# One square root a turn in the last stage of a convolution and attention kernel

## The chip, the core and the metric

The kernel runs on one core of a Trainium2 chip. A core has a matrix engine (PE, with weight loads shown apart as PEld), a vector engine (DVE), an activation engine (ACT), a general engine (POOL), a queue engine (SP) and 16 DMA engines. Each engine runs its own list of instructions in order, and waits on semaphores that the others raise. The metric is the device time of one execution in microseconds (us).

## What is computed

The input has 4 images of 64 channels and 256 x 256 pixels. Two layers follow each other. Only the end of the second one matters here: linear attention along the columns, then a small network at each pixel.

```
def _ln(x, g, b):
    m = x.mean(-1, keepdims=True)
    v = jnp.mean((x - m) ** 2, -1, keepdims=True)
    return (x - m) / jnp.sqrt(v + EPS_LN) * g + b
...
hc = _ln(h.swapaxes(1, 2), cn_g, cn_b)
h = h + _lin_attn(hc, col_wq, ..., col_bo).swapaxes(1, 2)
f = _ln(h, fn_g, fn_b)
f = gelu(f @ w1.T + b1) @ w2.T + b2
return moveaxis(h + f, -1, 1)
```

So `h` is normalized twice over its 64 channels: once before the attention, and once, after the attention has been added, before the network. Each normalization needs one square root and one reciprocal per pixel. In the attention, queries and keys have one channel for each of 4 heads; `elu(.) + 1` is applied to both, and elu needs an exponential.

## The kernel before, in words

The program is one function with several stages. Everything here happens in the last, `stage_d`. It works on 32 groups (4 images x 8). A group is a tile `h` of 128 partitions x 32 columns x 2 row halves x 64 channels, which `load` fetches with 4 DMAs of 512 KB on SP's queue (L1172); four such tiles exist at a time.

Four pieces of work run side by side, each for another group. In turn `n`:

- `scores(n+1)` transposes `h` in 8 pieces (`up`, L1210, copied by ACT at L1212), multiplies by the weights of queries and keys (L1219), and brings the products back with two transposes on DVE (L1224). The mean is inside the weights, so only the root is still to be applied: L1249. Then L1250 adds the bias, `feature` takes the smaller of the value and zero (L695) and its exponential (L696), L1258 makes `f`, and L1260 makes `kz`, the keys times the root.
- `result(n)` starts with the product of `kz` and `h` (L1271), goes through a chain of small steps (L1283 to L1299), and adds the attention to `h`: PE at L1305 and L1308, DVE at L1311. Then it normalizes the new `h` into four tiles `xf`.
- `turn` and `first`, for the group before, transpose a piece of `xf` (L1330, copied by ACT at L1332), multiply by the first weights (L1341) and apply the Gelu (L1343, four per piece).
- `second` transposes the piece of `h`, adds the second product (L1355 and L1358), and DVE evicts the sum to `st` (L1359). After 8 pieces four DMAs on POOL's queue write `st` out (L1365).

A turn has 8 steps, `r` = 0 to 7. In each step PE is given `turn(i+2)`, `first(i+1)`, a part of `scores`, a part of `result`, `second(i)`, and a part of `scores` and of `result` again, where `i = 8(n-1) + r`. `scores` and `result` are generators, and each `yield` ends a part. The first piece of `xf` of group `n` is transposed in step 6 of turn `n`; its second tile is needed from step 0 of the next turn.

PE's order is this order, written out by hand (`manual_schedule`). The orders of DVE and ACT are made by a planner that takes ready instructions by priority with its own estimate of the times. PSUM has 6 buffers called `mm` for nearly all products, and 2 called `sm`. A product that takes an `mm` buffer waits until the engine that reads the buffer's last content is done. So PE can be held by an eviction that has nothing to do with its own work.

The sum of a normalization is made by `spread`: for each of 2 tiles of 16 pixels x 64 channels the row sum (L1181, DVE), the centred values (L1183, DVE), their squares (L1185, ACT) and the sum of squares (L1189, DVE). `rstd` takes the root (L1194, ACT) and the reciprocal (L1196, DVE). ACT holds one table of functions at a time: going from Gelu to the root, to the exponential, or back shows in the trace as its own instruction, ACT_TABLE_LOAD.

In a turn before the change there are three calls of `rstd`: one of 64 values a partition for the scores, at the end of `scores`, and one of 32 for each half of the result.

Of the kernel before, what the change touches and what calls it, by code (L numbers as in the profile page):

```python
# [18 lines left out]
LN_S = 1.0 / C  # L19
# [230 lines left out]
def kernel(ctx: ExitStack, tc: tile.TileContext, x, packs, fd, out, off):  # L250
    nc = tc.nc
    B = x.shape[0]
    V, S, T, G, SY = nc.vector, nc.scalar, nc.tensor, nc.gpsimd, nc.sync
# [24 lines left out]
    eps_t = const.tile([128, 1], F32, name="eps_t")  # L278
# [18 lines left out]
    def bc(ap, n):  # L297

        return ap.unsqueeze(2).to_broadcast([ap.shape[0], ap.shape[1], n])
# [27 lines left out]
    p = sp1.enter_context(tc.tile_pool(name="pst", bufs=2))  # L327
    p1 = sp1.enter_context(tc.tile_pool(name="pst1", bufs=1))
# [110 lines left out]
    rss, l4s = {}, {}  # L439
# [699 lines left out]
    def stage_d():  # L1139
        with ExitStack() as cs:  # L1140
            p = cs.enter_context(tc.tile_pool(name="pd", bufs=2))
            p1 = cs.enter_context(tc.tile_pool(name="pd1", bufs=1))
# [25 lines left out]
            def load(b, g):  # L1168
                h = p.tile([128, 32, 2, C], F32, name="h", bufs=4)
                for rh in (0, 1):  # L1170
                    for j in (0, 1):
                        SY.dma_start(h[:, 16 * j:16 * j + 16, rh, :], hd[b, rh * 128:(rh + 1) * 128, :, 2 * g + j, :])  # L1172
                return h

            def spread(h, ks, v):

                xcs, sqs = [], []
                for k in ks:
                    src = h[:, 8 * k:8 * k + 8].rearrange("p c a e -> p (c a) e")
                    s1 = p.tile([128, 16], F32, tag="ln_s", name="ln_s")  # L1180
                    V.tensor_reduce(s1, src, AX.X, ALU.add)  # L1181
                    xc = p.tile([128, 16, C], F32, tag="xc", name="xc")
                    V.scalar_tensor_tensor(xc, bc(s1, C), -LN_S, src, ALU.mult, ALU.add)  # L1183
                    sq = p.tile([128, 16, C], F32, tag="ln_sq", name="ln_sq")
                    S.activation(sq, xc, AF.Square)  # L1185
                    xcs.append(xc)
                    sqs.append(sq)
                for i, k in enumerate(ks):
                    V.tensor_reduce(v[:, 16 * i:16 * i + 16], sqs[i], AX.X, ALU.add)  # L1189
                return xcs  # L1190

            def rstd(v, n):
                s3 = p.tile([128, n], F32, tag="ln_d", name="ln_d")
                S.activation(s3, v, AF.Sqrt, bias=eps_t, scale=LN_S)  # L1194
                s4 = p.tile([128, n], F32, tag="ln_r", name="ln_r")
                V.reciprocal(s4, s3)  # L1196
                return s4

# [3 lines left out]
            def scores(n):  # L1202
                h = hs[n]
                qp = p1.tile([128, 32, 32], F32, name="qp")
                v1 = p1.tile([128, 64], F32, name="v1")
# [24 lines left out]
                for r in range(8):  # L1230
                    if r == 0:
                        spread(h, (0, 1), v1[:, 0:32])
                    if r == 4:
                        back(0, qk)
                        qk = sm()
                    score(r, xT, qk)
                    if r < 7:
                        xT = up(r + 1)
                    if r == 3:
                        spread(h, (2, 3), v1[:, 32:64])  # L1240
                    yield
                    if r == 1:
                        yield
                        yield

                back(1, qk)
                rs = rstd(v1, 64)
                u = qp[:, :, 0:16].rearrange("p c (r k) -> p c r k", r=2)
                V.tensor_tensor(u, u, bc4(rs, 2, 8), ALU.mult)  # L1249
                V.tensor_tensor(u, u, cbq.unsqueeze(1).unsqueeze(1).to_broadcast([128, 32, 2, 8]), ALU.add)  # L1250
                e = feature(p1, u, [128, 32, 2, 8])
                yield
                f = p1.tile([128, 2, 2, 32, 4], F32, name="f")
# [6 lines left out]
                V.tensor_tensor(kz.rearrange("p r (c h) -> p r c h", h=4), f[:, :, 1], rs.rearrange("p (c r) -> p r c", r=2).unsqueeze(3).to_broadcast([128, 2, 32, 4]), ALU.mult)  # L1260
                fks[n] = f, kz

            def result(n):
                h = hs[n]
# [36 lines left out]
                for rh in (0, 1):  # L1301
                    ts = [mm() for g in range(4)]
                    for g in range(4):
                        r = slice(g * 32, g * 32 + 32)
                        T.matmul(ts[g], one[g * 32:g * 32 + 1, :], K("colbo8")[g * 32:g * 32 + 1, :], start=True, stop=False)  # L1305
                    for g in range(4):
                        r = slice(g * 32, g * 32 + 32)
# [3 lines left out]
                        V.tensor_tensor(hh, ts[g].rearrange("p (c e) -> p c e", c=8), hh, ALU.add)  # L1311
                    yield
                for hf in (0, 1):
                    v2 = p.tile([128, 32], F32, name="v2")
                    xcs = spread(h, (2 * hf, 2 * hf + 1), v2)
                    yield
                    rs = rstd(v2, 32)
                    for k in (0, 1):
                        xf = p.tile([128, 8, 2, C], F32, name="xf", bufs=6)
                        V.tensor_tensor(xf.rearrange("p c a e -> p (c a) e"), xcs[k], bc(rs[:, k * 16:k * 16 + 16], C), ALU.mult)  # L1320
                        xfs[n, 2 * hf + k] = xf
                    yield

            def turn(i):

# [9 lines left out]
            def first(i):  # L1335
                xT = xTs.pop(i)
                hgs[i] = []
                for k in (0, 1):
                    for rh in (0, 1):
                        t = mm()  # L1340
                        T.matmul(t, w1[rh * 64:(rh + 1) * 64, k * 128:(k + 1) * 128], xT[rh * 64:(rh + 1) * 64], start=True, stop=True)  # L1341
                        g = p.tile([128, 512], F32, tag=f"hg{rh}{k}", name=f"hg{rh}{k}")
                        S.activation(g, t, AF.Gelu, bias=b1[:, k:k + 1])  # L1343
                        hgs[i].append(g)
# [22 lines left out]

            seq = [(b, g) for b in range(B) for g in range(8)]
            N = len(seq)
            hs, fks, xfs, xTs, hgs, sts = {}, {}, {}, {}, {}, {}  # L1370
            hs[0] = load(*seq[0])
            with tc.manual_schedule(engines={mybir.EngineType.PE}):
                for n in range(-1, N + 1):
                    if 0 <= n + 2 < N:
                        hs[n + 2] = load(*seq[n + 2])
                    gs = scores(n + 1) if n + 1 < N else iter(())
                    gr = result(n) if 0 <= n < N else iter(())
                    for r in range(8):
                        i = 8 * (n - 1) + r
                        if 0 <= i + 2 < 8 * N:  # L1380
                            turn(i + 2)
                        if 0 <= i + 1 < 8 * N:
                            first(i + 1)
                        next(gs, 0)
                        next(gr, 0)
                        if 0 <= i < 8 * N:
                            second(i)
                        next(gs, 0)
                        next(gr, 0)
                    _steps(gs, gr)  # L1390

    stage_d()


# [18 lines left out]
```

## Time and profile before

| what | value |
|---|---|
| time, median of 3 runs | 8800.12 us (8797.13 to 8805.94) |
| the profiled execution's own time | 8803.6 us, span 8801.8 us |
| its granted PE clock, mean | 0.969 of full speed |
| PE busy | 8178.1 us (93%) |
| DVE busy | 5927.4 us (67%) |
| ACT busy | 4601.7 us (52%) |
| last stage | from about 6690 us to the end |
| 30 turns in it, 6824.20 to 8728.50 us | 1904.3 us, 63.48 us each |

How to read it: a busy PE is not a PE at its peak, since a matmul that waits inside the pipeline counts as busy. Shares of the whole span mix stages with different limits; what matters here is one turn of the last stage. Times in the trace are counted from the start of the span. Releasers ("<-DVE kz L1260") say which instruction ended a wait. The granted clock is 1.00 at full speed and 0.50 at half.

### The profile page before, as it was taken

To read this page: it belongs to the slowest core of one execution; us is meant where nothing else is said; L and a number is where in the kernel's file an instruction comes from. 1 tells how busy PE (TensorE), PEld (TensorE's weight loads), DVE (VectorE), ACT (ScalarE), POOL (GpSimd) and SP (SyncE) were. 2 spreads that over 40 slices of the span, in tenths; PEclk is the share of its full clock that TensorE was granted. 3 is DMA by queue.
4 is the path that set the end of the run, shared out by engine and by line. 5 is a ranking of instruction groups with operands and counts; after the bars stand their busy time and mean duration, and the time that the engine had idled before them with its cause. 6 is when DMAs were issued, how large, how long until landed. Compare 5 with 4: busy or idle time off the path is not lost. (4 is left out here: it accounts for less than half of the span.)

```text
span 8801.8 us, 143151 instructions
## 1 busy us (share of the span) xinstructions
PE 8178.1 (93%) x57518; PEld 4216.6 (48%) x57518; DVE 5927.4 (67%) x8506; ACT 4601.7 (52%) x7779; POOL 1205.2 (14%) x1828
## 2 busy tenths in 40 slices
PE   8999999699999998999999999999997999999998
PEld 6777777344444443333333344444443444444443
DVE  7766666377777774222222288888886888888886
ACT  4455455455555553222222266666663777777776
POOL 1111111212222221000000011111110010101011
PEclk9999999699999999999999999999997999999999
DMA  7777777799999998888888755555552232323232
GB/s 161 161 188 187 182 182 180 193 347 388 396 391 388 386 387 320 298 296 298 296 297 298 273 184 172 173 168 167 169 158 63 59 77 58 77 58 77 58 77 39
DMA packets 1258502, 1832.48 MB, mean 208 GB/s; under 512 B 335600, under 2 KB 1040112, under 8 KB 1196656
## 3 DMA queue, kind: packets, MB, share of 16 engines
q1 hardware_dynamic: 1053296, 1034.63, 39.0%
q0 software_dynamic: 204544, 788.69, 28.0%
q8 instruction: 456, 7.47, 0.3%
q14 instruction: 206, 1.69, 0.1%
HBM read 967.65 MB, written 788.53 MB: 200 GB/s over the span
## 5 line engine op out<-in xcount | busy, mean ns | idle before, releaser
L915 DVE TENSOR_TENSOR y<-ge,mm 128x512 f32<-128x512 f32 (+1 forms) x640 | 406.3, 635 | 1212.8 <-ACT ge L914 1212.8
L882 PE MATMUL mm<-t,w 128*128 128x512 f32 (+1 forms) x2560 | 1094.1, 566 | 18.8 <-DMA t<-td 18.8
L914 ACT ACTIVATE ge<-mm 128x512 f32<-128x512 f32 (+1 forms) x640 | 354.9, 555 | 1253.5 <-PE mm L889 1253.5
L775 PE MATMUL mm<-gp,wc 128*64 128x510 f32 (+1 forms) x3072 | 702.7, 596 | 90.8 <-DVE xm L785 51.4
L620 PEld LDWEIGHTS mm<-wqk,gp 128*128 128x128 f32 x6144 | 728.7, 197 | 99.2 <-issue 61.5
L882 PEld LDWEIGHTS mm<-t,w 128*128 128x128 f32 x2560 | 455.4, 190 | 647.5 <-issue 437.0
L620 PE MATMUL mm<-wqk,gp 128*128 128x128 f32 x6144 | 762.3, 282 | 1.1 <-POOL gp L589 0.9
L1341 PE MATMUL mm<-xfT,w 64*128 64x512 f32 x2048 | 620.9, 642 | 51.1 <-ACT hg L1343 26.8
L1343 ACT ACTIVATE hg<-mm,b 128x512 f32<-128x512 f32 x1024 | 634.1, 688 | 53.2 <-PE mm L1341 51.5
L830 ACT COPY tb<-mm 128x512 f32<-128x512 f32 x512 | 300.7, 588 | 632.4 <-PE mm L824 632.1
L889 PE MATMUL mm<-t,w 64*64 64x504 f32 (+1 forms) x5120 | 575.6, 555 | 0.0
L824 PE MATMUL mm<-xl,pack_c 64*128 64x512 f32 x2048 | 513.5, 601 | 8.1 <-ACT xl L812 4.7
L1358 PE MATMUL mm<-hg,pack_d 128*64 128x512 f32 x2048 | 505.8, 615 | 0.0
L775 PEld LDWEIGHTS mm<-gp,wc 128*64 128x64 f32 x3072 | 277.8, 137 | 470.5 <-issue 333.3
L316 ACT ACTIVATE ln_sq<-xn 128x1024 f32<-128x1024 f32 x256 | 274.3, 1072 | 365.4 <-DVE xn L314 365.3
L1365 POOL DMA_DIRECT2D out_dram<-st x128 | 209.1, 1638 | 1756.3 <-DVE fe L695 1543.6
L318 DVE TENSOR_REDUCE ln_v<-ln_sq 128x16 f32<-128x1024 f32 x256 | 312.0, 1219 | 186.0 <-ACT ln_sq L316 186.0
L970 PE MATMUL mm<-ya,pack_e 128*64 128x512 f32 x1024 | 381.2, 616 | 11.2 <-DMA ya<-yd 11.2
L828 DVE COPY tb<-mm 128x512 f32<-128x512 f32 x512 | 345.0, 685 | 24.0 <-PE mm L824 18.5
L1359 DVE TENSOR_SCALAR st<-mm,pack_d 128x512 f32<-128x512 f32 x256 | 281.1, 1098 | 117.9 <-PE mm L1358 117.6
L1341 PEld LDWEIGHTS mm<-xfT,w 64*128 64x128 f32 x2048 | 225.1, 192 | 276.1 <-issue 125.7
L1185 ACT ACTIVATE ln_sq<-xc 128x1024 f32<-128x1024 f32 x256 | 273.0, 1067 | 132.1 <-DVE xc L1183 132.1
(458 smaller groups left out, 15283.8 us busy)
## 6 DMA issues: line engine op xcount, KB each, us to landing
t<-td SPq DMA_DIRECT2D x256, 1152.0 KB, 9.9
td<-tb POOLq DMA_DIRECT2D x144, 1024.0 KB, 15.6
td<-tb POOLq DMA_DIRECT2D x288, 512.0 KB, 13.9
yd<-y POOLq DMA_DIRECT2D x128, 1152.0 KB, 10.1
ya<-yd SPq DMA_DIRECT2D x192, 512.0 KB, 5.7
xs<-in_x_dram SPq DMA_DIRECT2D x128, 512.0 KB, 6.8
projd<-pj POOLq DMA_DIRECT2D x256, 256.0 KB, 6.0
gp<-projd SPq DMA_DIRECT2D x128, 512.0 KB, 9.5
```

Of the source, the lines that this page charges most:

```text
L620: T.matmul(qp[:, k * 128:(k + 1) * 128], gp[:, 2 * i + k // 2, at + dx:at + dx + 128], wqk[:, dx, :], start=(dx == 0), stop=(dx == 2))
L775: T.matmul(tv[i * 64:(i + 1) * 64, :, o], wc[2 * pr + i][:, dx, :], gps[i][:, 2 * r:2 * r + 2, i_], start=(dx == 1), stop=False, skip_grou ...
L824: T.matmul(t, inT[q, hf * 128:(hf + 1) * 128], xls[b // 2, s][q, :, 2 * y:2 * y + 2].rearrange("p f y t -> p f (y t)"), start=True, stop=True)
L828: V.tensor_copy(o, i_)
L882: T.matmul(t[:, :n], w[:, 0:128], x_[:, c, :], start=True, stop=False, skip_group_check=True)
L889: T.matmul(t[po:po + 64, :n].rearrange("p (n c) -> p n c", c=64)[:, :, o], w[q:q + 64, 128:192], x_[q:q + 64, c, i_], start=False, stop=Tr ...
L914: S.activation(ge[:, :n], ts[0][k][:, :n], AF.Gelu)
L915: V.tensor_tensor(y[:, c, :].rearrange("p n c -> p (n c)"), ge[:, :n], ts[1][k][:, :n], ALU.mult)
L970: T.matmul(t[b * 64:(b + 1) * 64, :], owT, ya[:, :, 2 * r:2 * r + 2, b * 64:(b + 1) * 64].rearrange("p f y t -> p y f t"), start=True, sto ...
L1341: T.matmul(t, w1[rh * 64:(rh + 1) * 64, k * 128:(k + 1) * 128], xT[rh * 64:(rh + 1) * 64], start=True, stop=True)
L1343: S.activation(g, t, AF.Gelu, bias=b1[:, k:k + 1])
L1358: T.matmul(y[rh * 64:(rh + 1) * 64, :], w2[:, k, :], hg[k * 2 + rh], start=False, stop=(k == 1), skip_group_check=True)
```

## The change

`scores` and `result` no longer take roots. A tile `v1` of 128 values a partition holds the sums of squares of a turn: 64 for the scores of group `n+1`, and 64 for the result of group `n`. `root(n, ...)`, called in step 5 of turn `n` before that step's parts of `scores` and `result`, takes one root and one reciprocal of all 128 values.

The sums for the scores of group `n+2` are made in steps 6 and 7 of turn `n`, after everything else of these steps, so that they are complete one turn ahead; those of group 0 come before the loop. The sums for the result stay in steps 3 and 4, and the centred values are written straight into `xf`. All four `xf` tiles are multiplied by the root in place, in step 5, after `root`. There `result` has two empty parts before. No DMA is added or removed, and PE has the same products in the same order.

```
-            def spread(h, ks, v):
-
-                xcs, sqs = [], []
-                for k in ks:
+            def spread(h, ks, v, xcs=None):
+
+                sqs = []
+                for i, k in enumerate(ks):
...
-                    xc = p.tile([128, 16, C], F32, tag="xc", name="xc")
+                    xc = xcs[i].rearrange("p c a e -> p (c a) e") if xcs else p.tile([128, 16, C], F32, tag="xc", name="xc")
...
-            def rstd(v, n):
-                s3 = p.tile([128, n], F32, tag="ln_d", name="ln_d")
-                S.activation(s3, v, AF.Sqrt, bias=eps_t, scale=LN_S)
-                s4 = p.tile([128, n], F32, tag="ln_r", name="ln_r")
-                V.reciprocal(s4, s3)
-                return s4
+            def root(n, lo, hi):
+
+                s3 = p1.tile([128, 128], F32, tag="ln_d", name="ln_d")
+                S.activation(s3[:, lo:hi], vs[n][:, lo:hi], AF.Sqrt, bias=eps_t, scale=LN_S)
+                rss[n] = p.tile([128, 128], F32, tag="ln_r", name="ln_r")
+                V.reciprocal(rss[n][:, lo:hi], s3[:, lo:hi])
+
+            def variances(n):
+                if n not in vs:
+                    vs[n] = p.tile([128, 128], F32, name="v1")
+                return vs[n]
...
-                    if r == 0:
-                        spread(h, (0, 1), v1[:, 0:32])
...
-                    if r == 3:
-                        spread(h, (2, 3), v1[:, 32:64])
...
-                rs = rstd(v1, 64)
+                rs = rss[n - 1][:, 0:64]
...
                 for hf in (0, 1):
-                    v2 = p.tile([128, 32], F32, name="v2")
-                    xcs = spread(h, (2 * hf, 2 * hf + 1), v2)
+                    xf = [p.tile([128, 8, 2, C], F32, name="xf", bufs=6) for k in (0, 1)]
+                    spread(h, (2 * hf, 2 * hf + 1), variances(n)[:, 64 + 32 * hf:96 + 32 * hf], xf)
+                    for k in (0, 1):
+                        xfs[n, 2 * hf + k] = xf[k]
                     yield
-                    rs = rstd(v2, 32)
-                    for k in (0, 1):
-                        xf = p.tile([128, 8, 2, C], F32, name="xf", bufs=6)
-                        V.tensor_tensor(xf.rearrange("p c a e -> p (c a) e"), xcs[k], bc(rs[:, k * 16:k * 16 + 16], C), ALU.mult)
-                        xfs[n, 2 * hf + k] = xf
-                    yield
+                yield
+                yield
+
+                for k in range(4):
+                    xf = xfs[n, k].rearrange("p c a e -> p (c a) e")
+                    V.tensor_tensor(xf, xf, bc(rss[n][:, 64 + k * 16:80 + k * 16], C), ALU.mult)
+                    if k % 2:
+                        yield
...
             hs[0] = load(*seq[0])
+            for k in (0, 1):
+                spread(hs[0], (2 * k, 2 * k + 1), variances(-1)[:, 32 * k:32 * k + 32])
...
+                        if r == 5 and n < N:
+                            root(n, 0 if n + 1 < N else 64, 128 if 0 <= n < N else 64)
                         next(gs, 0)
                         next(gr, 0)
                         if 0 <= i < 8 * N:
                             second(i)
                         next(gs, 0)
                         next(gr, 0)
+                        if r > 5 and n + 2 < N:
+
+                            k = r - 6
+                            spread(hs[n + 2], (2 * k, 2 * k + 1), variances(n + 1)[:, 32 * k:32 * k + 32])
```

More of the change, by code (lines that the diff above doesn't have):

```diff
@@ L1185, in spread @@
                     S.activation(sq, xc, AF.Square)
-                    xcs.append(xc)
                     sqs.append(sq)
@@ L1189, in spread @@
                     V.tensor_reduce(v[:, 16 * i:16 * i + 16], sqs[i], AX.X, ALU.add)
-                return xcs
-            def rstd(v, n):
-                s3 = p.tile([128, n], F32, tag="ln_d", name="ln_d")
-                S.activation(s3, v, AF.Sqrt, bias=eps_t, scale=LN_S)
-                s4 = p.tile([128, n], F32, tag="ln_r", name="ln_r")
-                V.reciprocal(s4, s3)
-                return s4
+            def root(n, lo, hi):
[7 more added lines that the diff above has]
+                return vs[n]
             def scores(n):
@@ L1204, in scores @@
                 qp = p1.tile([128, 32, 32], F32, name="qp")
-                v1 = p1.tile([128, 64], F32, name="v1")
                 def up(r):
@@ L1369, in stage_d @@
             N = len(seq)
-            hs, fks, xfs, xTs, hgs, sts = {}, {}, {}, {}, {}, {}
+            hs, fks, xfs, xTs, hgs, sts, vs, rss = {}, {}, {}, {}, {}, {}, {}, {}
             hs[0] = load(*seq[0])
+            for k in (0, 1):
+                spread(hs[0], (2 * k, 2 * k + 1), variances(-1)[:, 32 * k:32 * k + 32])
             with tc.manual_schedule(engines={mybir.EngineType.PE}):
```

## The prediction

> **What bounds the kernel now.** I read the page first, then the stretches of one turn of the last stage, then the instructions of that turn in order of time on each engine. The page says where the engines stand over all stages, which settles nothing here: DVE is at 67% of the whole span. One turn, from the first row sum of the result (L1181, 8019.98) to the next one (8083.14), is cut where `kz` (L1260) is ready, at 8062.77:
>
> ```profile
> 8019.98:8083.14 63.16, 57.73 (x350) 26.25 (x350) 54.31 (x67) 47.85 (x70) 6.63 (x5) 1.00 0.34 67
> 8019.98:8062.77 42.79, 37.50 (x212) 16.52 (x211) 42.03 (x49) 37.14 (x52) 3.01 (x2) 1.00 0.24 53
> 8062.77:8083.14 20.37, 20.23 (x138) 9.73 (x139) 12.28 (x19) 10.72 (x19) 3.62 (x4) 1.00 0.56 97
> ```
>
> The columns are length, then busy time of PE, PEld, DVE, ACT and POOL, the granted clock, DMA share and GB/s. In the first 42.8 us DVE never stops (42.03); in the last 20.4 us PE doesn't (20.23). So a turn is a DVE stretch of 42.8 us, in which ACT and PE follow DVE, and then a PE stretch of 20.4 us. An edit shortens the turn if it brings forward the end of the DVE stretch, and if PE can use that.
>
> ACT's table loads stand in the DVE stretch:
>
> ```profile
> 8047.94 1.28 ACT L1194 ACT_TABLE_LOAD   x1
> 8049.24 0.32 ACT L1194 ACTIVATE ln_d<-v,eps_t 128x32 f32<-128x32 f32 x1
> 8049.57 1.28 ACT L1343 ACT_TABLE_LOAD   x1
> 8050.87 0.69 ACT L1343 ACTIVATE hg<-mm,b 128x512 f32<-128x512 f32 x1
> 8051.57 1.28 ACT L1194 ACT_TABLE_LOAD   x1
> 8052.87 0.35 ACT L1194 ACTIVATE ln_d<-v,eps_t 128x64 f32<-128x64 f32 x1
> 8053.12 0.57 ACT L1332 COPY xfT<-mm 128x512 f32<-128x512 f32 x1
> 8053.71 1.28 ACT L1343 ACT_TABLE_LOAD   x1
> ```
>
> Two roots of one turn, 3.6 us apart, with a Gelu between them: four loads. The same gap on PE, in this turn and in the one before it:
>
> ```profile
> 8051.61 1.12 PE L1341 MATMUL mm<-xfT,w 64*128 64x512 f32 x2 [1.42 <-ACT hg L1343]
> 8053.25 1.94 PE L1358 MATMUL mm<-hg,pack_d 128*64 128x512 f32 x8
> 8062.91 1.50 PE L1271 MATMUL mm<-h,kz 128*32 128x512 f32 x12 [0.99 <-DVE kz L1260]
> ...
> 7986.67 1.85 PE L1341 MATMUL mm<-xfT,w 64*128 64x512 f32 x2 [1.43 <-ACT hg L1343]
> 7989.50 3.68 PE L1358 MATMUL mm<-hg,pack_d 128*64 128x512 f32 x8
> ```
>
> After the gap at 7986 the eight L1358 took 3.68 us instead of 1.94: the granted clock was 0.50 there for about 7 us, and that turn lasted 64.95 us (from 7967.77 to 8032.72, between equal instructions) where the next lasted 63.15. Four of the 30 turns counted have it; the mean of 63.48 over 63.16 makes some 10 us in all.
>
> **The change part by part.** I count in us from the first row sum of the result (zero is 8019.98 or 8083.14), with the order in which the changed program issues its instructions.
>
> *Table loads.* In the order of the built program the last stage goes from 251 loads (95 for L1194, 124 for L1343, 32 for L696) to 128, that is four fewer a turn, and from 96 roots to 33. At 1.283 us a load and 0.32 a root: 4 x 1.283 + 2 x 0.32 = 5.8 us less ACT a turn, 180 us in all. [...]
>
> *DVE's stretch.* The three reciprocals (0.33, 0.33 and 0.56) become one of 128 values; from 32 to 64 values the row grows by 0.23, so 1.0 is my estimate, a wash. What counts is what the new order puts ahead of `kz`. A row sum, a centring, a sum of squares and a scaling each take 1.13 from start to start, an eviction (L1359) 0.95, an L1224 0.61, an L1249 or L1250 0.6, L695 0.35, the four L1258 0.93, L1260 0.43. The new list up to `kz`: first row sum and three additions 2.9; then 13 of the 1.13 kind with one eviction and one L1224 up to the last sum of squares, where it is 18.05; eviction, centring, row sum, reciprocal: 22.2; one centring, and the first `xf` is scaled at 24.4; the other three with an eviction 28.6; L1224, two sums of squares, L1249, L1250 and an eviction 33.6; L695 34.0; two row sums 36.2; L1258 37.1; a centring 38.3; `kz` 38.7; and then the eviction of step 7 at 39.65. So `kz` is ready 4.1 us earlier than before (42.8): one centring and two sums of squares now stand behind it, and two short waits on ACT are gone.
>
> *What PE makes of it.* The moved root is in step 5, and ACT is given it ahead of that step's four Gelus. It waits for the last of all four sums of squares (18.05), which DVE reaches one after another; before, the Gelus waited for a half. Load, root and load back end at 20.3, the Gelus at 22.7 and the copy of `xT` behind them at 23.2. PE ends step 5 at 21.6 and sits until 23.3 (1.65), does 0.36 us of scores, and sits until 24.5 (0.85) for the first `xf`, which before was ready 7.6 us ahead of its use (8035.08 for 8042.67). Steps 6 and 7 then run to 34.3 (before: 35.1). In step 0 the third product of `first` needs the buffer of step 7's third Gelu. That one stands on ACT behind the exponential, which waits for L695 (34.0), and behind the load back: 34.1 + 0.64 + 1.28 + 0.67 = 36.7. And `up` needs the buffer that step 7's eviction frees, at 39.65, because on DVE that eviction is queued behind the exponential's consumer, a centring and `kz`. PE idles 0.95 and then 2.0 us. With `up` at 39.75, `second` (2.45) ends at 42.75, and only there does the product with `kz` (L1271) start. Before it started at 42.93. So of 4.1 us, 0.2 reach the product: 31 turns x 0.2 = 6 us less. My list has some 32 terms, each good to 0.02 or so: 0.6 us a turn either way, 19 us in all.
>
> Nothing else is on the path. The sums for group n+2 read an `h` that was loaded a turn earlier (issued at 8053.35, landed 5.5 us later, first read about 45 us after that), so SP's queue isn't touched; POOL's stores keep their place; `xf` has six buffers, and none of its new, earlier writers waits for PE in the built program. The last turn has no scores: its first `xf` comes at about 18.5, where PE asks for it at 18.0, so 0.5 us. If the buffer for `up` came free in time, see the third case.
>
> *The clock.* The new gaps are longer and lie closer together than the one that tripped it. Step 6: 0.36 us of work in 2.9 us. Step 0: 0.96 us of work in 3.9 us. [...] A trip in step 6 delays the Gelus ahead of the exponential: 0.8 to 2.3 us, I take 1.2. One in step 0 makes `up` and `second` (2.95 us) at half speed, in the PE stretch: 1.6 to 3.4, I take 1.9. Sum: 0.38 x 1.2 + 0.31 x 1.9 = 1.05 us a turn, 32 us, bounded by nothing and by (2.3 + 3.4) x 31 = 177 us. The old gap in step 7 goes, about 10 us with it, most of that.
>
> Sum against the profiled execution's 8803.6: -6 - 9 + 32 + 8 = +25. The 8 is for the start of the stage, where the clock is at half (0.50 from 6680 to 6764) and the changed order puts two row sums and a centring ahead of `kz`: 3 x 1.13 = 3.4 us in each of the first two turns, about 7, and 0.5 at the end. The profiled time is 3.5 us over the median, a difference that the runs themselves have (8797 to 8806). So 8800 + 25 = 8825.
>
> **The rivals.**
> *No difference.* The clock doesn't trip at the new gaps. Then -6 - 9 + 8: 8793. [...] Against: the trips at 1.43.
> *Faster.* One mechanism: the step 7 eviction gets to PE earlier than my list has it, because DVE's order leaves it room before `kz`, so `up` is not held. Then `up` follows the fourth product at 37.8, `second` ends at 40.7, and L1271 starts 2.2 us earlier than before: 31 x 2.2 = 68 us, 8735; if PE is on time throughout, 4.1 x 31 = 127, 8675. It decides if that eviction ends before 37.8 instead of 39.65. For it: 5.8 us less ACT in a stretch where ACT is on the chain of waits. Against: the order of the built program.
> *Much slower.* Half clock at both gaps in nearly every turn: 3.1 us, less the old trips, 31 x 2.9 = 90: 8890.
>
> **How the numbers follow.** Forecast 0.43, no difference 0.19, faster 0.25, much slower 0.13. The forecast's own range is 8805 to 8860. A measurement of this kernel can tell 0.2%, 17.6 us. Faster than 8782.5: the faster case and a little of the second, 0.27. Same: most of the second and the low edge of the forecast, 0.18. Slower: 0.55. For 8 in 10 I go from 8740, leaving out half of the faster case, to 8890, leaving out half of the much slower one.
>
> **What would show it.** Loads down to 128, ACT about 42 us of a turn. `kz` at 38.7 from the first row sum, and L1271 within 0.6 of 42.75. PE idle ahead of the L1330 of step 6 with xf's scaling as the releaser, and ahead of the L1210 of step 0 with the eviction as the releaser. More stretches of clock 0.50, at these two places. The prediction is wrong if L1271 starts before 41, or if the granted clock of the stage doesn't fall below the 0.98 of before.

## The result, and the profile after

| what | before | after |
|---|---|---|
| median of 15 runs each | 8796.94 us (8791.59 to 8807.71) | 8781.35 us (8775.92 to 8789.75) |
| ratio, 95% interval | | 0.9981 (0.9973 to 0.9989) |
| span of the profiled execution | 8801.8 us | 8779.0 us |
| PE clock of the profiled execution, mean | 0.969 | 0.971 |
| ACT busy | 4601.7 us | 4429.7 us |
| table loads in the last stage | 251 | 128 |

The forecast was 8825, slower. The kernel became 16 us faster by the medians, and 22.8 us in the two profiled executions. The interval of the ratio leaves out 1, so there is a gain, but it is no larger than the 0.2% that the prediction took as the least that can be told from no change.

The same three stretches of a turn as the prediction shows, from the first row sum of the result (L1181, 7118.24) to the next, cut where `kz` (now L1258) is ready; columns as there:

```profile
7118.24:7180.97 62.73, 56.73 (x350) 25.54 (x350) 53.58 (x65) 42.30 (x64) 6.63 (x5) 1.00 0.34 68
7118.24:7156.79 38.55, 33.62 (x196) 14.55 (x195) 38.55 (x44) 29.62 (x43) 0.00 (x0) 1.00 0.15 34
7156.79:7180.97 24.18, 23.12 (x154) 10.99 (x155) 15.03 (x22) 12.68 (x22) 6.63 (x5) 1.00 0.65 122
```

`kz` is ready 38.55 us after the first row sum instead of 42.79, and ACT has 5.5 us less to do. Of these 4.2 us, 0.4 reach the end of the turn (62.73 for 63.16). DVE again never stops until `kz`; but now PE stands still at four places. ACT's only root of the turn, and then PE of the same turn:

```profile
7135.60 1.28 ACT L1193 ACT_TABLE_LOAD   x1
7136.90 0.40 ACT L1193 ACTIVATE ln_d<-v,eps_t 128x128 f32<-128x128 f32 x1
7137.32 1.28 ACT L1345 ACT_TABLE_LOAD   x1
7138.61 2.42 ACT L1345 ACTIVATE hg<-mm,b 128x512 f32<-128x512 f32 x4
7140.91 0.60 ACT L1214 COPY xT<-mm 128x512 f32<-128x512 f32 x1
```

```profile
7141.57 0.43 PE L1221 MATMUL sm<-xT,cwt 128*32 128x128 f32 x8 [1.64 <-ACT xT L1214]
7142.64 0.66 PE L1332 MATMUL mm<-pack_k,xf 128*128 128x128 f32 x4 [0.65 <-DVE xf L1322]
...
7154.99 1.70 PE L1343 MATMUL mm<-xfT,w 64*128 64x512 f32 x4 [0.71 <-ACT hg L1345]
7157.85 0.66 PE L1212 MATMUL mm<-pack_k,h 128*128 128x128 f32 x4 [1.17 <-DVE st L1361]
7158.35 0.60 PE L1357 MATMUL mm<-pack_k,h 128*128 128x128 f32 x4
7158.88 1.94 PE L1360 MATMUL mm<-hg,pack_d 128*64 128x512 f32 x8
7160.74 1.92 PE L1269 MATMUL mm<-h,kz 128*32 128x512 f32 x16
```

The prediction had 1.65, 0.85, 0.95 and 2.0 us for these four waits; they are 1.64, 0.65, 0.71 and 1.17. It had `up` at 39.75 and the product with `kz` at 42.75; they start at 39.61 and 42.50. So the walk along the order was right almost to a tenth, but for the last wait, which is 0.8 us shorter than foreseen. What was wrong is what the half clock makes of these waits. A stretch in which the granted clock is 0.50 is called a trip below. Here is the turn before it, where it strikes in step 0, and the one before that, where it strikes in step 6:

```profile
7090.62 1.70 PE L1343 MATMUL mm<-xfT,w 64*128 64x512 f32 x4 [0.71 <-ACT hg L1345]
7093.49 0.92 PE L1212 MATMUL mm<-pack_k,h 128*128 128x128 f32 x4 [1.18 <-DVE st L1361]
7094.21 1.06 PE L1357 MATMUL mm<-pack_k,h 128*128 128x128 f32 x4
7095.20 2.88 PE L1360 MATMUL mm<-hg,pack_d 128*64 128x512 f32 x8
7098.02 1.92 PE L1269 MATMUL mm<-h,kz 128*32 128x512 f32 x16
```

```profile
7014.47 0.43 PE L1221 MATMUL sm<-xT,cwt 128*32 128x128 f32 x8 [1.65 <-ACT xT L1214]
7015.54 1.11 PE L1332 MATMUL mm<-pack_k,xf 128*128 128x128 f32 x4 [0.64 <-DVE xf L1322]
7016.59 2.99 PE L1343 MATMUL mm<-xfT,w 64*128 64x512 f32 x8
...
7028.97 1.70 PE L1343 MATMUL mm<-xfT,w 64*128 64x512 f32 x4 [0.34 <-ACT hg L1345]
7030.76 0.66 PE L1212 MATMUL mm<-pack_k,h 128*128 128x128 f32 x4
...
7033.65 1.92 PE L1269 MATMUL mm<-h,kz 128*32 128x512 f32 x16
```

In step 0 the trip costs 1.64: the product with `kz` starts 44.14 after the turn's first row sum (7053.88) instead of 42.50. In step 6 L1332 and L1343 lose 1.45 us (1.11 for 0.66, 2.99 for 1.99), and the product still starts 42.48 after the first row sum (6991.17). PE gets there late, and the two waits of step 0 shrink by as much: 0.71 to 0.34, 1.17 to nothing the profile lists. The eviction for which PE waits comes from DVE, and DVE did not wait for PE up to there: `kz` is ready 38.49 to 38.55 us after the first row sum in all 29 turns counted below, with a trip or without.

In what follows a turn is counted from one `bdm` (now L1297) to the next, and the 29 turns without the first and the last of the stage are called steady. The kernel after has 13 steady turns with a trip in step 6 (62.74 us on average), 9 with none (62.71), and 7 with one in step 0 (64.34). Before there were 25 of 63.24 on average and 4 of 64.94.

Free trips were there before the change too. The prediction counted only the four turns of 64.9, but 15 of the 25 others have one trip of 3.41 us each and take 63.28 on average, against 63.17 for the 10 without. Here is one, in the turn right after the one that the prediction walked through:

```profile
8098.67 0.43 PE L1219 MATMUL sm<-xT,cwt 128*32 128x128 f32 x8 [2.00 <-ACT xT L1212]
8099.03 0.66 PE L1210 MATMUL mm<-pack_k,h 128*128 128x128 f32 x4
8099.52 1.00 PE L1330 MATMUL mm<-pack_k,xf 128*128 128x128 f32 x4
8100.45 3.23 PE L1341 MATMUL mm<-xfT,w 64*128 64x512 f32 x8
```

The same L1341 takes 2.06 us one turn earlier, after the same wait of 2.00. So this wait trips the clock in some turns and not in others, and the trip reaches the end of the turn with 0.1 us only.

The 22.8 us come together like this:

| part | us |
|---|---|
| 29 steady turns without costly trips: 62.73 for 63.24 | -14.8 |
| costly trips: 7 x 1.61 for 4 x 1.70 | +4.5 |
| earlier stages, which are the same in both kernels | -2.6 |
| start of the stage: 0.5 up to the first `bdm`, 6.9 in the turn after it | -7.4 |
| last turn -6.9, after it +4.3 | -2.5 |

The first transposes of the last stage start at 6689.90 after and at 6692.55 before. Over the 13 traces of this document that moment lies between 6683.4 and 6692.6, so these 2.6 us are no gain of the change.

### The profile page after: what moved, and what is told of

The parts are those of the page before. It is cut to its first block, busy times and chain, and to the rows that moved or that the text cites. A ratio compares the mean times of both kernels' runs of the same rounds, so it can differ in the third digit from the quotient of the medians.

```text
span 8779.0 us, 142778 instructions
## 1 busy us (share of the span) xinstructions
PE 8140.2 (93%) x57518; PEld 4195.8 (48%) x57518; DVE 5915.0 (67%) x8443; ACT 4429.7 (50%) x7593; POOL 1205.3 (14%) x1828
## 5 line engine op out<-in xcount | busy, mean ns | idle before, releaser
L1343 PE MATMUL mm<-xfT,w 64*128 64x512 f32 x2048 | 594.8, 643 | 40.8 <-DVE h L1309 22.6
L1360 PE MATMUL mm<-hg,pack_d 128*64 128x512 f32 x2048 | 503.5, 613 | 0.0
L1361 DVE TENSOR_SCALAR st<-mm,pack_d 128x512 f32<-128x512 f32 x256 | 282.3, 1103 | 131.7 <-PE mm L1360 131.7
L889 PEld LDWEIGHTS mm<-t,w 64*64 64x64 f32 x5120 | 158.1, 132 | 374.4 <-issue 374.4
L812 ACT ACTIVATE xl<-mm,pack_c 128x256 f32<-128x256 f32 x512 | 334.8, 815 | 0.8 <-PE mm L810 0.8
```

The costliest lines, as they stand in the source:

```text
L889: T.matmul(t[po:po + 64, :n].rearrange("p (n c) -> p n c", c=64)[:, :, o], w[q:q + 64, 128:192], x_[q:q + 64, c, i_], start=False, stop=Tr ...
L1360: T.matmul(y[rh * 64:(rh + 1) * 64, :], w2[:, k, :], hg[k * 2 + rh], start=False, stop=(k == 1), skip_group_check=True)
L1361: V.tensor_scalar(st[:, :, 4 * r:4 * r + 4].rearrange("p r c -> p c r"), y.rearrange("p (c r) -> p c r", c=4), K("b2"), None, ALU.add)
```

## The experiments

Times are medians; the ratio is to the kernel before, run in turn with it, with its 95% interval. "Undisturbed" is the length of the steady turns in which no trip costs anything; in the runs with the sums ahead, the root of the result alone and step 7 evicted by ACT nearly every turn has a trip, and the shortest common length stands there. Turns are those of one profiled execution of each run.

| run | us | ratio | undisturbed turn | longer turns of 29 |
|---|---|---|---|---|
| kernel before | 8797 | 1 | 63.2 | 4 of 64.9 |
| kernel after | 8781.35 | 0.9981 (0.9973, 0.9989) | 62.7 | 7 of 64.3 |
| before, no root functions | 8789.21 | 0.9989 (0.9982, 0.9995) | 62.4 | 16 of 64.0, 2 of 63.2 and 63.4 |
| after, no root function | 8764.83 | 0.9961 (0.9948, 0.9973) | 62.7 | none |
| sums ahead, three roots | 8799.34 | 1.0001 (0.9993, 1.0009) | 63.5 | 8 of 63.7 to 63.9, 9 of 64.0, 3 of 64.7 (all 29 with trips) |
| root of the result alone | 9036.12 | 1.0270 (1.0256, 1.0284) | 71.7 | all alike, the clock halves in each |
| step 7 evicted by ACT | 8879.45 | 1.0093 (1.0079, 1.0107) | 66.2 | about half of 66.9 |
| `kz` behind the eviction | 8772.07 | 0.9968 (0.9955, 0.9980) | 62.5 | 17 of 62.6 to 62.8, 3 of 64.1 |
| and `up` to an sm buffer | 8760.16 | 0.9956 (0.9943, 0.9968) | 62.0 | 12 of 62.5 to 62.8, 2 of 64.1 |
| half of the sums late | 8754.42 | 0.9949 (0.9937, 0.9962) | 61.7 | 13 of 62.8 to 63.0, 1 of 63.9 |
| after, step 0 filled | 8775.80 | 0.9975 (0.9965, 0.9985) | 62.7 | 14 of 63.0 to 63.2, 1 of 64.5 |
| half late, step 5 filled with 4 | 8773.24 | 0.9971 (0.9959, 0.9984) | 62.2 | 18 of 62.8 to 63.3 |
| half late, step 5 filled with 2 | 8745.92 | 0.9942 (0.9928, 0.9955) | 61.7 | 6 of 62.7 to 63.0 |

**Are the table loads the price?** First the roots alone are taken out, in each kernel: the instruction stays, as an identity, and ACT needs no load for it.

```
-                S.activation(s3, v, AF.Sqrt, bias=eps_t, scale=LN_S)
+                S.activation(s3, v, AF.Identity, bias=eps_t, scale=LN_S)
```

> The kernel before with its roots of the last stage taken as an identity of the same size (the square root is left out), which needs no table load: 188 of its 251 loads go, six a turn. Theory A (a turn is DVE's list up to kz, then a PE stretch; loads matter only where DVE or PE ends up waiting for ACT): L1271 moves by less than 1 us a turn, the half-clock stretch of step 7 goes with its gap, and the shortened waits of the first and last turns come on top: 10 to 45 us less than before, so about 8755 to 8787. Theory B (the loads are on the path and their number sets the time): six loads of 1.283 us in 31 turns, 240 us less, about 8560; at half of that 8680.

> The changed kernel with its one root a turn taken as an identity (the square root is left out): the last two loads a turn for roots go. Theory A: the Gelus of step 5 come 1.3 us earlier, but step 6 then waits for the first scaled xf, which DVE's list sets (24.4 from the first row sum), and up of step 0 waits for the eviction of step 7 as before: 0 to 8 us less than the changed kernel, about 8775 to 8781. Theory B: 66 loads fewer at 1.283 us, 85 us less, about 8696; at the 0.19 us a load that the change itself shows, 13 us less, 8769.

Before loses 188 loads of 1.283 us, 241 us of ACT, and gains 9 us, a little less than theory A's least. An undisturbed turn is 0.8 shorter, since `kz` is ready 0.9 earlier (41.88 for 42.79), but 16 turns trip in step 0, which theory A did not foresee. After loses 65 loads and gains 16 us, more than theory A had and near the weaker form of theory B, but with the same undisturbed turn (62.7); what it gains is that no steady turn trips. The four waits of PE there:

```profile
7014.71 0.43 PE L1221 MATMUL sm<-xT,cwt 128*32 128x128 f32 x8 [1.53 <-ACT xT L1214]
7015.07 0.66 PE L1332 MATMUL mm<-pack_k,xf 128*128 128x128 f32 x4
...
7026.99 2.86 PE L1343 MATMUL mm<-xfT,w 64*128 64x512 f32 x8 [0.83 <-ACT hg L1345]
7031.06 0.66 PE L1212 MATMUL mm<-pack_k,h 128*128 128x128 f32 x4 [1.22 <-DVE st L1361]
```

The wait for `xf` in step 6 is gone; those for ACT's copy and for the eviction have stayed. So in the kernel after no load and no root is on the path of an undisturbed turn. In the kernel before the roots with their loads were worth 0.8 us a turn, which is 25 us in 31 turns and not 241. The number of loads alone does not give the time.

**One half of the change at a time.** The sums one turn ahead, in the kernel before with its three roots, and then the one root for the four tiles of the result, with sums and root of the scores as they were:

```
-                    if r == 0:
-                        spread(h, (0, 1), v1[:, 0:32])
...
+                        if r > 5 and n + 2 < N:
+                            k = r - 6
...
+                            spread(hs[n + 2], (2 * k, 2 * k + 1), vs[n + 2][:, 32 * k:32 * k + 32])
```

> The kernel before with one part of the change: the sums of squares for the scores are made in steps 6 and 7 of the preceding turn; the three roots a turn stay where they were, so that the table loads stay too. Theory A (what brings kz forward is DVE's order, not the loads): DVE's list up to kz is as short as in the changed kernel, 38.7 plus waits for ACT; the time is 8770 to 8797, that is most of the change's gain without any load saved, unless the three roots' loads make DVE wait. Theory B (the loads made the gain): the same as before, 8797, or slower.

```
-                        if r == 5 and n < N:
-                            root(n, 0 if n + 1 < N else 64, 128 if 0 <= n < N else 64)
+                        if r == 5 and 0 <= n < N:
+                            root(n, 64, 128)
...
+                S.activation(s3, v1, AF.Sqrt, bias=eps_t, scale=LN_S)
```

> One root of 64 values for the result in step 5; the sums and the root of the scores stay where they were in the kernel before. 64 loads more than the changed kernel has, 62 fewer than before. Theory A (an undisturbed turn follows DVE's list up to kz and the eviction of step 7, and loads are off the path): the list up to kz is about as long as before, 42 us, so the turn stays within 0.3 us of 63.2 and the time at 8790 to 8806. Theory B (each root taken away is worth a fixed part of the gain): two thirds of the roots removed are gone here too, so about 8786. Where the clock trips in step 0 the time can be up to 1.6 us x 30 = 48 us above A.

The sums alone: nothing, where theory A had up to 27 us. They shorten the first turn (56.6 us for 65.3) and lengthen the steady ones. `kz` is ready at 39.0 to 39.8 in nearly all of them (42.8 before), and still the product with `kz` starts at 43.2 to 43.8 (42.93 before). Every steady turn of this run has trips, so how long one without would be is not known. The root alone costs 236 us, which neither theory expected:

```profile
7034.61 2.31 DVE L1188 TENSOR_REDUCE v<-ln_sq 128x16 f32<-128x1024 f32 x2
...
7044.24 1.21 DVE L1330 TENSOR_TENSOR xf<-xf,ln_r 128x1024 f32<-128x1024 f32 x1
```

```profile
7030.55 1.28 ACT L1251 ACT_TABLE_LOAD   x1
7033.02 2.19 ACT L1185 ACTIVATE ln_sq<-xf 128x1024 f32<-128x1024 f32 x2 [0.83 <-DVE xf L1183]
7035.24 1.28 ACT L1353 ACT_TABLE_LOAD   x1
```

```profile
7037.27 1.12 PE L1365 MATMUL mm<-pack_k,h 128*128 128x128 f32 x4 [5.12 <-ACT hg L1353]
7038.32 3.42 PE L1368 MATMUL mm<-hg,pack_d 128*64 128x512 f32 x8
7045.50 1.11 PE L1340 MATMUL mm<-pack_k,xf 128*128 128x128 f32 x4 [3.40 <-DVE xf L1330]
7046.55 3.79 PE L1351 MATMUL mm<-xfT,w 64*128 64x512 f32 x8
```

The turn's first row sum is at 7013.18. As in the kernel after, all four sums of squares of the result come before the first scaled tile, but here the sums of the scores, of the same turn, stand between them: the last is done after 23.7 us (18.1 in the kernel after), the first scaling starts after 31.1 (23.1). PE waits twice: 5.12 us for a Gelu, which stands on ACT behind the root of the scores (L1251), two squares and the load back, and 3.40 us for the first `xf`. Both times it then runs at half clock (L1368 3.42 for 1.94, L1351 3.79 for 1.99). Counting DVE's list up to `kz` only had missed that. So table loads do stand in PE's way in this order, and the 236 us are not the price of the late sums alone; the shares were not separated. The sums ahead pay for the late root, and in the one run that has them without it they earned nothing in a steady turn.

**The eviction that holds `up`.** The third rival says that 68 us and more are to be had if step 7's eviction does not hold `up`. One run gives that eviction to ACT:

```
+                if r == 7:
+                    S.activation(st[:, :, 4 * r:4 * r + 4].rearrange("p r c -> p c r"), y.rearrange("p (c r) -> p c r", c=4), AF.Identity, bias=K("b2"))
```

> The changed kernel with one eviction of eight, that of step 7, made by ACT instead of DVE, so that the buffer that up of step 0 takes is freed without DVE's queue. Theory A (up is held by DVE's place for that eviction, and the clock drop of step 0 comes from this gap): up starts some 1.9 us earlier, L1269 with it, DVE's list is 1 us shorter behind kz, and the slow stretches of step 0 go: 31 x 1.9 + 10, some 60 to 75 us less than the changed kernel, about 8710. Rival (up isn't what holds the turn; the exponential and the Gelus behind it are): 0 to 20 us less, 8760 to 8781. Rival (the eviction delays the Gelus of step 0 on ACT): slower than the changed kernel.

```profile
7034.76 1.16 ACT L1362 ACTIVATE st<-mm,pack_d 128x512 f32<-128x512 f32 x1
7035.70 2.02 ACT L1185 ACTIVATE ln_sq<-xc 128x1024 f32<-128x1024 f32 x2
7037.59 0.60 ACT L1334 COPY xfT<-mm 128x512 f32<-128x512 f32 x1
```

```profile
7035.98 0.66 PE L1212 MATMUL mm<-pack_k,h 128*128 128x128 f32 x4
7038.24 1.11 PE L1357 MATMUL mm<-pack_k,h 128*128 128x128 f32 x4 [1.61 <-ACT xfT L1334]
7039.29 3.06 PE L1360 MATMUL mm<-hg,pack_d 128*64 128x512 f32 x8
```

It is slower, as the second of the two rivals said, though the wait is not the one that this rival named. `up` no longer waits. But `second` does, for a copy that stands on ACT behind the eviction and two squares; and the clock halves there (L1360 3.06 for 1.94). The wait was moved to another engine's queue and came back longer. The next two runs leave ACT alone: first `f` and `kz` are written two parts later, so that DVE evicts ahead of `kz`; then, as well, `up` of step 0 writes to an sm buffer.

```
                 e = feature(p1, u, [128, 32, 2, 8])
                 yield
+                yield
+                yield
```

> The changed kernel, with f and kz written two parts later, so that DVE evicts step 7 ahead of kz instead of behind it, 0.41 us earlier; kz itself is 1.1 us later. Theory A (PE is held in step 0 by that eviction, not by kz): 0.4 us x 31 = 13 us less, and the trips of the clock in step 0, 7 of 1.6 us, go or get fewer: 8758 to 8770, with the wait of the transposes of h on st down from 0.92 to about 0.5. Theory B (the eviction isn't what sets the turn; something else holds PE there): no change, 8776 to 8788. If kz counts: above 8790.

```
-                    t = mm()
+                    t = mm() if r else sm()
```

> As the one with f and kz later, and the first transposes of h in step 0 write to one of the two sm buffers, so that they wait for no eviction; the next to need the mm buffer of step 7 is second, 0.66 us of work later. Theory A: PE starts the transposes at once and second about 0.7 us earlier than in the changed kernel, 0.7 x 31 = 22 us, and no trip of the clock in step 0, 11 us: 8746 to 8762. Theory B (something else holds PE): 8776 to 8788. Rival C: the products of the result wait for the sm buffer until ACT has copied it, which is 0.6 us after the product with kz starts, and PE stands there instead: 8780 to 8800.

Both show that the eviction is what holds PE: the undisturbed turn goes from 62.7 to 62.5 and then to 62.0, the time from 8781 to 8772 and 8760 (the interval of the first still touches that of the kernel after, the second's does not). The first gains half of what was expected (0.2 for 0.4 us a turn): `up` starts 0.36 earlier, and the product with `kz` 0.19. And something comes in with it that the kernel after did not have: turns with a trip in step 6 are now longer than the others, by up to 0.2 us in the first (1.5 in three turns) and 0.6 to 0.8 in the second. The wait that hid these trips has been used up.

**Half of the sums in the stretch where DVE is idle.** The row sums of half of the scores' tiles are written to the tile of `z`, so that they cannot come ahead of `zn`:

```
+                    s1 = p1.tile([128, 64], F32, tag="z", name="z")[:, 0:16] if late else p.tile([128, 16], F32, tag="ln_s", name="ln_s")
...
+                        if r == 1 and n + 1 < N:
+                            spread(hs[n + 1], (0, 1), variances(n)[:, 0:32], late=True)
+                        if r == 7 and n + 2 < N:
+                            spread(hs[n + 2], (2, 3), variances(n + 1)[:, 32:64])
```

> The changed kernel, with half of the sums of the scores (6.8 us of DVE a turn) made in the stretch in which PE is the bound and DVE stands idle for 8 us: their row sums are written to the tile of z, so they come after zn. Theory A (a turn is a DVE stretch and a PE stretch, and what counts of the moved sums is what of them stands ahead of the eviction of step 7): three of their operations, 3.4 us, no longer stand ahead of that eviction; the transposes of step 0 no longer wait for it, PE gets there up to 2.2 us earlier as in the faster rival, and gives about 1 us of it back because bdm comes later: 1.0 to 2.2 us x 31 = 31 to 68 us less, and the trips of step 0 gone: 8700 to 8750. Theory B (PE or ACT is the bound of the first stretch too): 8770 to 8790. Rival C: the later bdm holds PE for the whole of what DVE puts in ahead of it, 2.5 us: 8790 to 8830.

```profile
7021.25 0.90 DVE L1256 SCALAR_TENSOR_TENSOR f<-qp,fe 128x128 f32<-128x128 f32 x4 [1.89 <-ACT fe L696]
7022.18 0.42 DVE L1258 TENSOR_TENSOR kz<-f,ln_r 128x256 f32<-128x256 f32 x1
7022.52 1.09 DVE L1361 TENSOR_SCALAR st<-mm,pack_d 128x512 f32<-128x512 f32 x1
7027.73 1.10 DVE L1361 TENSOR_SCALAR st<-mm,pack_d 128x512 f32<-128x512 f32 x1 [4.12 <-PE mm L1360]
```

The lines are DVE's, ahead of the product with `kz`, which starts at 7027.61. DVE now waits for ACT and for PE, and step 7's eviction (7022.52) is over 1.1 us before `up` asks for its buffer (7024.73). The undisturbed turn is 61.7, 1.0 less than in the kernel after, the low end of what was expected, and a trip in step 6, which 13 turns have, makes a turn 1.1 to 1.3 us longer (one of them 2.2). There the trip does what the prediction said: it delays the Gelus ahead of the exponential, and `kz` is ready at 37.3 instead of 36.1. The time, 8754, is just outside.

**The clock by itself.** If too little work around a wait lets the clock fall, work that nobody needs should hold it. In the kernel after, the first transposes of step 0 are made twice, into the wait for the eviction; in the kernel with half of the sums late, the scores of one piece are repeated in step 5, four times or twice.

```
+                    if r == 0:
+                        t = sm()
+                        for i in range(4):
+                            T.transpose(t[:, i * 128:(i + 1) * 128], h[:, r * 4 + i].rearrange("p a e -> p (a e)"), ident)
```

> The changed kernel with the first four transposes of h in step 0 made twice, the first time into an sm buffer that nobody reads: 0.66 us more work for PE, put into the stretch of 0.92 us in which it waits for the eviction of step 7. Theory A (in the changed kernel 7 turns of 29 lose 1.6 us because the work around this wait is too little to hold the full clock, and an undisturbed turn is set by DVE): the 7 long turns become 62.7, 11 us less, undisturbed turns unchanged: 8764 to 8772. Theory B (the long turns have another reason, or PE's added work is on the path): 8779 to 8800.

```
+                    if r == 7:
+                        for k in range(4):
+                            score(6, xT6, qk)
```

> The kernel with half of the sums of the scores made late, and in step 5 the scores of piece 6 made five times instead of once, into the same place and with the same values: about 1.5 us more work for PE in the 1.65 us in which it waits for xT. Theory A (with DVE's stretch shortened, PE's clock in step 6 now counts: in that kernel 13 of 29 turns are 62.8 to 63.0 and one 63.9, the others 61.7): with the wait filled the clock stays up, all turns are 61.7, 13 x 1.2 + 2.2 = 18 us less: 8734 to 8744. Theory B (the 62.9 has nothing to do with step 6): 8752 to 8760. If the filling overruns the wait, up to 0.3 us a turn more than A.

> As the run with the wait in step 5 filled, but the scores of piece 6 are made three times instead of five: some 0.7 us more work for PE in the 1.65 us, and a shorter filling for which the planner keeps the orders of ACT and DVE in a turn as they are without filling (with the longer one it had moved one Gelu a turn). Theory A (the trips in step 6 cost 1.2 us in 13 turns there, and the longer filling lost because a Gelu was moved and because zn then falls into the time in which POOL issues a store): 0.9 + 0.36 + 0.65 us of gaps with work between them hold the clock, turns are 61.7 throughout, 8736 to 8744. Theory B (the filling itself costs, or 0.7 us of work is too little to hold the clock): 8750 to 8760 with the same 62.8 to 63.0 turns, or 8760 to 8775 if more work on PE is what made the turns longer.

In step 0 the filling does what was expected of it: the seven turns of 64.3 are gone. But 15 turns trip in step 6, and these are now 0.3 to 0.5 us longer, one of them 1.8: the 0.66 us of filling stand in the wait that would have hidden them. So the time, 8776, lies between the two theories. The four repetitions in step 5 end the trips in step 6 too, and the kernel is still 19 us slower than without them. In the order of the built program one Gelu a turn had moved (`up` in step 0 comes 0.45 later), and in 18 turns `zn` is held like this, on DVE and on POOL:

```profile
7530.37 1.25 DVE L706 TENSOR_SCALAR hm<-pack_k,qr 128x4 f32<-128x4 f32 x1
7530.56 1.10 DVE L1292 TENSOR_SCALAR zn<-z,rz 128x64 f32<-128x64 f32 x1
7531.69 1.22 DVE L1181 TENSOR_REDUCE z<-h 128x16 f32<-128x1024 f32 x1
```

```profile
7530.02 1.63 POOL L1371 DMA_DIRECT2D out_dram<-st  x1 [2.83 <-issue]
```

`zn` takes 0.25 us elsewhere; here it ends when POOL's issue of the fourth store ends (7531.65). With two repetitions the orders of ACT and DVE in a steady turn stay as they were, four turns trip in step 6 instead of 13, `zn` is held in two, and 8745.92 us, just above what was expected, is the lowest of all medians: 0.9942 (0.9928 to 0.9955) of the kernel before, with the same output computed. The interval overlaps that of the version without filling, so that it is the fastest rests on the medians and on the turns of one profile each. Four trips are left, so in these profiles 0.7 us of work makes them rarer without ending them.

## Why the prediction was wrong

**Loads and roots.** Right: 128 loads, 33 roots, 172 us less of ACT (180 foreseen), and from a load to the root behind it are 1.30 us (7135.60 to 7136.90). That ACT, busy for 47.85 of the 63.16 us of a turn before, isn't the bound is shown by the two runs without root functions: 241 us less of ACT gave 9, and the undisturbed turn of the kernel after did not move.

**DVE's stretch and what PE makes of it.** Right in its steps (`kz` at 38.55 for 38.7, the product at 42.50 for 42.75, all four waits with the releasers named), and short in its sum: -0.2 us a turn was within 0.6, as it said, and came as -0.43 between these two turns, -0.5 on average. (It counts 13 operations of 1.13 us up to 18.05; its sum, and the trace, have 12.) That is 9 of the 48 us between the +25 of the sum and the -22.8 of the two profiles.

**The clock.** An error of 18 us. The forecast put trips in step 6 in 0.38 of the turns and in step 0 in 0.31, shares that no run shows. In the profile of the kernel after they are in 13 of 29 (0.45) and 7 of 29 (0.24). Each in step 0 costs 1.61 (1.9 foreseen). The step that failed is "A trip in step 6 delays the Gelus ahead of the exponential: 0.8 to 2.3 us, I take 1.2". It delays PE by 1.45 us and costs 0.03 a turn, since in a turn bound by DVE PE's delay is taken out of a wait that comes later. The prediction had that wait in its own list (`up` held to 39.75) and did not set it against the delay. Nor did it see the 15 nearly free trips of the kernel before: the wait of 2.00 us at 8033.5 trips nothing, and one turn later the same wait trips the clock and costs 0.1. So +32 was +11, and with the old trips gone +4.5 for +23. That the same trip costs 1.2 us once the wait is used up was shown by the runs with `up` freed and with half of the sums late. The new gaps trip the clock, as the forecast expected: no single gap of PE in a steady turn of the kernel after is longer than 1.65 us, but for one of 1.92, and the clock fell in 20 turns of 29.

**Start and end.** Foreseen +8, measured -9.9, without the 2.6 us of the earlier stages: 18 us, as much as the clock. In the kernel before, PE's first product with `kz`:

```profile
6787.15 3.64 PE L1271 MATMUL mm<-h,kz 128*32 128x512 f32 x16 [14.22 <-DVE kz L1260]
```

It waited 14.22 us and ran at half clock (3.64 for 1.92). After, it starts at 6781.20, takes 1.92, and does not wait for `kz`; PE's long wait of that turn is 10.50 us for the first `xf`, where it was 2.72 before. The step that failed is "the changed order puts two row sums and a centring ahead of `kz`: 3 x 1.13 = 3.4 us in each of the first two turns": in the first turn the whole sums of its scores have moved away from `kz`, and the run with the sums ahead and the roots unchanged shows the same gain (56.6 for 65.3 in that turn), while the run with the sums in place and no root functions keeps 64.9. The 0.5 us for the last turn was wrong as well: the one root comes later than half a root, and PE waits 4.62 us in the last turn of the result, with a trip behind it:

```profile
8710.79 1.12 PE L1332 MATMUL mm<-pack_k,xf 128*128 128x128 f32 x4 [4.62 <-DVE xf L1322]
```

The turn ahead of it is 6.9 us shorter: no sums are left there to be made ahead, and its own were made a turn earlier. The same shows in the run with the sums ahead alone, 61.3 for 64.4. Seen as a whole, 13.6 us of DVE's work (12 operations of 1.13) have left the loop for the time before it, where they cost nothing (44.3 us from the first transposes of the stage to the first `bdm`, 44.7 before). The forecast had counted what the moved sums put in the way, and not that the last such turn has none.

**The rivals.** "No difference", 8793, was nearest, for a wrong reason: the clock does trip. "Faster" was right in its mechanism, but the change doesn't do it; only the versions with the eviction ahead of `kz` or with half of the sums late do, and they give 9 to 27 us of the 68 it had, without filling. (Its 8735 is 8803.6 less 68, where the other cases are counted from 8800.) "Much slower" did not come: trips are in 20 turns of 29, and 13 of them are free. By the prediction's own last sentence it was wrong: the clock of the stage (6830 to 8640) is 0.98 before and after.

## What to carry over

Before a stall is added to a sum, look for the next wait of the same engine that another engine ends: a delay ahead of it is free up to its length, and it stops being free in the version that removes that wait. A change of two halves should be costed as a whole and in halves; here the halves alone, as the planner ordered them, give 0 and +236 us, and together -16. And the first and last turn of a loop need a walk of their own: with 32 turns they were worth about as much as all the others.

## What was not expected of the hardware

- Trips of the clock recur in a pattern. After the change a turn of 64.3 us is followed by one without a trip, then two with a trip in step 6, and by the next of 64.3, many times over: 62.73, 62.76, 62.71 and 64.33 us make 252.5 us. That is 74 times 3.41. In the traces of the kernels before and after every stretch between two changes of the granted clock, at 1.00 or at 0.50, lasts a whole multiple of 3.413 us, and each of the 20 trips in the steady turns of the kernel after lasts one; so the changes stand on a grid that runs on through the turns. Why 16 steady turns have a costly trip in one of the two runs without root functions and none in the other was not shown, and what share of work around a wait makes the clock fall was not measured.
- Two small DVE instructions (a product by a scalar, of 4 and of 64 values a partition) take up to 1.14 and 1.29 us in the kernel before, for 0.22 and 0.25, when POOL is issuing a store, and end with it. Others do not: in the kernel after the row sum L1283 takes 1.02 us beside such an issue and 1.01 elsewhere, and the eviction L1361, a TENSOR_SCALAR too, 1.11 and 1.10. Why those two and not these was not shown. In the kernel before 25 of the 29 steady turns have it, in the kernel after the 7 with a trip in step 0. It cost nothing in the kernel after: from the product with `kz` to the next first row sum are 20.2 us with it and without. It cost 0.6 to 1.2 us a turn in the run where 18 turns had it.
